# Keys and values of the first layer by node type, and table rows sent by indirect writes

## The chip, the cores and the metric

The kernel runs on one NeuronCore of a Trainium2 chip. The metric is the device time of one execution in microseconds (us), the median of several runs. A core has five engines that run side by side, each with its own queue of instructions in a fixed order: TensorE (PE, matrix products; PEld is its loading of weights), VectorE (DVE), ScalarE (ACT), GpSimd (POOL) and SyncE (SP, which only sends transfers here). Transfers between DRAM and the on-chip memory run on 16 DMA engines; they are sent from SyncE's queue (hardware_dynamic in the profile) or, where addresses come from data, from GpSimd's (software_dynamic: indirect gathers and indirect writes).

## The reference

A graph with N = 6250 nodes of 128 features and E = 200,000 edges sorted by target, with 16 node types and 32 edge types (RT), goes through two layers of attention over the edges with 8 heads of 16 features. `typed_linear` is a product whose matrix depends on the node's type.

```python
k = typed_linear(x, ntype, Wk).reshape(n, H, HS)
q = typed_linear(x, ntype, Wq).reshape(n, H, HS)
v = typed_linear(x, ntype, Wv).reshape(n, H, HS)
kT = jnp.einsum('nhd,htdo->nhto', k, Watt)
vT = jnp.einsum('nhd,htdo->nhto', v, Wmsg)
kw = kT[src, :, etype]
m = vT[src, :, etype]
a = jnp.einsum('ehd,ehd->eh', kw, q[dst]) * pri[:, etype].T / SQRT_D
att = edge_softmax(a, dst, n)
msg = (m * att[:, :, None]).reshape(-1, H * HS)
hag = jax.ops.segment_sum(msg, dst, num_segments=n)
h = jax.nn.silu(typed_linear(hag, ntype, Wa))
alpha = jax.nn.sigmoid(skip[ntype])[:, None]
h = h * alpha + x * (1.0 - alpha)
...
return (h - mu) * jax.lax.rsqrt(var + 1e-05) * g + b
```

After both layers come a product with `ff_w`, the addition of x and a normalization of each row.

## The kernel before

The nodes are cut into 49 tiles of 128. For each layer a table in DRAM holds, for every node and every edge type, the node's key and value under that edge type, 256 numbers; the table of layer 0 has one number more in each row, 32 times the node's place in the order by degree plus the edge type (1028 bytes a row, 206 MB in all). The edges of a target are then served by gathers out of that table (`gather`, L921): one indirect gather fetches one row for each of 128 targets into the tile `ring`.

The change touches what stands in front of the first such gather. Four pieces of it matter:

- **The edge check.** `load_edges` (L343 on) loads the edges, compares each target with its neighbour and sums the violations into `flag`; all engines load `flag` (L889) and branch over a sort that these inputs don't need. The first line behind the branch is the cast of `bounds` (L893).
- **The preparation.** `prepare` (from L510) finds each node's first edge: POOL writes the comparison tiles `cols` (L526), VectorE makes `less` from them (L531), TensorE counts, and `blk_i` (L541) names the block in which a node's edges begin. POOL gathers these blocks into `part` (L550, 50 gathers), VectorE compares them (`lt`, L558) and sums (`begin`, L560). Nodes are then ranked by degree: a 0/1 tile `hot` of 64 bins by 49 tiles (L599), two rounds of products into `total` and `ahead`, a running sum (L618), three passes over 3136 columns (L620 to L625). The places `pos_f` go to DRAM (`posd`) and come back turned, and `places` makes `place32` out of them (L507); from then on tables can be numbered. The records of all nodes are brought into that order by 49 pairs of `here` and `what` (L651, L653) with a product each, and `rec` is what POOL's gathers of `xg` (L683, x rows in that order, stored as `xperm`) and `idx_all` (L693, edge lists) read.
- **The typed keys and values.** `first_typed` and `one_typed` work on groups of two tiles: rows and types are loaded, transposed (L413), and for each of 16 types VectorE makes a masked copy `xm` (L426) and TensorE adds two products, with `wk` and `wv`, to one bank `kv` (L441). The groups run beside the preparation and beside the tables.
- **The tables.** `first_tables` goes over groups and tiles; for each tile `table_rows` makes 16 products of 512 columns (L474) with the relation blocks `bk`, `bv`, and ScalarE and VectorE copy each into a stage `st` (L483). A stage holds half a tile's rows, and there are four. VectorE writes the numbers (L847), and `send` sends each stage with two plain transfers of 1028 KB from SyncE (L872).

The program is written out by a planner. Each piece is a thread that yields an engine, a duration and what it waits for; the planner keeps a clock for every engine and emits the step that can begin first, ties going to the lower number in `RANK`. So the order of instructions on each engine is fixed by planned times; only the waits are settled on the chip. `relation_blocks` loads `bk`, `bv` and the scales `pr` by 24 small transfers and multiplies `bk` by `pr` on VectorE (L329, L330). `first_states` writes two DRAM tiles `state` from `init` (L878). The planner of the ring stage starts anew behind all this, with its own clock.

Of the kernel before, what the change touches and what calls it, by code (L numbers as in the profile page):

```python
# [31 lines left out]
F32 = mybir.dt.float32  # L32
# [6 lines left out]
P = 128  # L39
# [6 lines left out]
GL = 2  # L46
# [7 lines left out]
AHEAD = 2  # L54
KEPT = 16
STAGES = 4
# [11 lines left out]
RANK = dict(table=0, empty=0, gather=1, attend=1.6, prepare=2, mask=3, typed=3, late=4, query=1, behind=1.2, masks=1.4, early=1.8)  # L68
# [164 lines left out]
def gnn_kernel(ctx: ExitStack, tc: tile.TileContext, x, src, dst, etype, ntype, Wk, Wq, Wv, Wa,  # L233
# [17 lines left out]
    GROUPS = [list(range(a, min(a + GL, NTILE))) for a in range(0, NTILE, GL)]  # L251
# [86 lines left out]
    wk, wv = (load_typed(first, n, w[0]) for n, w in (("wk", Wk), ("wv", Wv)))  # L338
# [7 lines left out]
    def load_edges():  # L346

        landed = []
        for name, ap, fill in (("dst_i", dst, NODST), ("src_i", src, 0), ("typ_i", etype, 0)):
            us = yield "DVE", 1.4, ()  # L350
            edges[name] = t = pp.tile([P, EC], I32, tag=name, name=name)
            nc.vector.memset(t, fill)
# [39 lines left out]
        nc.sync.dma_start(out=csort[NBLK : NBLK + 1], in_=pad)  # L392

# [8 lines left out]
    def load_group(pool, tag, ap, t0, n, bufs):  # L402
        t = pool.tile([P, n, P], F32, tag=f"{tag}{n}", name=tag, bufs=bufs)
        nc.sync.dma_start(out=t, in_=ap[t0 * P : (t0 + n) * P].rearrange("(j p) d -> p j d", p=P))
        return t

    zeros = first.tile([P, GT * P], BF16, tag="zeros", name="zeros")
    nc.vector.memset(zeros, 0.0)

    def transposed(t, rows, n, needs):  # L410
        us = yield "PE", Work(n * P), needs
        for j in range(n):
            nc.tensor.transpose(t[:, j * P : (j + 1) * P], rows[:, j], ident)  # L413
        return t, us

    def typed(pool, tag, xT, types, M, cols, rows, opens, ends, clear, needs):


        ready, busy = [When() for _ in range(NT)], [When() for _ in range(NT)]
        masks, last = {}, [0.0]  # L420

        def mask():
            for t in range(NT):
                us = yield "DVE", dve_us(M), [*needs, busy[t - XM] if t >= XM else 0.0]
                xm = pool.tile([P, M], F32, tag=f"{tag}{M}", name=tag, bufs=XM)
                nc.vector.scalar_tensor_tensor(xm, types[:, :M], float(t), xT[:, :M], op0=ALU.is_equal, op1=ALU.mult)  # L426
                masks[t], ready[t].us, last[0] = xm, us, us

        plan.spawn(mask(), RANK["mask"])
        for t in range(NT):  # L430
            busy[t].us = yield "PE", Work(M * (len(cols) + len(rows))), [ready[t], clear]
            xm = masks.pop(t)
            if t == 0:
                for a in opens:
                    nc.tensor.matmul(a, zeros[:, :P], zeros[:, : a.shape[-1]], start=True, stop=False)
            todo = [(w, acc[:, :M], None) for w, acc in cols]
            todo += [(w, acc[:, c : c + P], slice(c, c + P)) for w, acc in rows for c in range(0, M, P)]
            for i, (w, to, c) in enumerate(todo):
                last_of = t == NT - 1 and i in ends
                if c is None:  # L440
                    nc.tensor.matmul(to, w[:, t], xm, start=False, stop=last_of)  # L441
                else:
                    nc.tensor.matmul(to, xm[:, c], w[:, t], start=False, stop=last_of)
        return busy[-1].us, last[0]

    def copied(pool, tag, acc, M, bufs, needs):
        us, e = yield ("ACT", "DVE"), (act_us(M), dve_us(M)), needs
        t = pool.tile([P, M], F32, tag=f"{tag}{M}", name=tag, bufs=bufs)
        if e == "ACT":
            nc.scalar.copy(t, acc[:, :M])  # L450
        else:
            nc.vector.tensor_copy(t, acc[:, :M])
        return t, us
# [35 lines left out]
    ap = early.enter_context(tc.tile_pool(name="ap", bufs=2))  # L489
# [3 lines left out]
    placed, known, searched = When(), When(), When()  # L493
# [7 lines left out]
    def places(posn, got):  # L501

        us = yield "PE", Work(P), [got]
        to = tabs[0]
        nc.tensor.transpose(to[:, :NTILE], posn, ident[:NTILE, :NTILE])
        us = yield "DVE", 0.3, [us]
        nc.vector.tensor_scalar(place32, to[:, :NTILE], float(RT), None, op0=ALU.mult)  # L507
        known.us = us

    def prepare():  # L510
        stage = ExitStack()
# [5 lines left out]
        yield "DVE", 0.3, ()  # L517
        ones_b = pp.tile([P, P], BF16, tag="ones_b")
        nc.vector.memset(ones_b, 1.0)
# [22 lines left out]
        searched.us = us  # L542
        begin = pp.tile([P, NC1], F32, tag="begin")
        seen = [us]
        for t0 in range(0, NC1, CB):
# [3 lines left out]
            for t in range(n):  # L549
                nc.gpsimd.indirect_dma_start(  # L550
                    out=part[:, t], out_offset=None, in_=dsort,
                    in_offset=bass.IndirectOffsetOnAxis(ap=blk_i[:, t0 + t : t0 + t + 1], axis=0),
                    bounds_check=NBLK - 1, oob_is_err=False)
# [19 lines left out]
        yield "SP", 1.6, ()  # L573
        nt_i = pp.tile([P, NTILE], I32, tag="nt_i")
        full = N // NTILE
        nc.vector.memset(nt_i, -1)
        nc.sync.dma_start(out=nt_i[:112], in_=ntype[: 112 * NTILE].rearrange("(p t) -> p t", t=NTILE))
# [980 lines left out]
```

## Time and profile before

| what | us |
|---|---|
| median of 3 runs | 6403.71 (6397.04 to 6416.18) |
| the profiled execution | 6422.69 |
| its span in the trace | 6420.9 |
| from the start to `blk_i` | 64.9 |
| first sends of the table | 216.89 |
| first gather into the ring | 879.07 |
| from there to the end | 5541.8 |

In rows of the trace a line names an instruction by engine, line, operation and tile (`out<-in`), with its duration; [ ] at its end holds how long the engine was idle before it and what ended the wait. A row "x8" joins eight instructions that follow each other. The granted clock (PEclk) is the share of TensorE's full speed that the chip granted in a stretch: 1.00 is 2.4 GHz and 0.5 is 1.2 GHz. A DMA share is the mean busy share of the 16 DMA engines.

### The profile page before, as it was taken

The numbers are of one execution on the slowest core, as the hardware profiler recorded it, in microseconds if no ns is written. First come the engines' busy times: TensorE is split into PE (matmuls) and PEld (weight loads), VectorE is DVE, ScalarE is ACT, GpSimd is POOL, SyncE is SP. The second block draws the span as 40 slices with busy tenths as digits, with TensorE's granted clock in tenths as the row PEclk, the third lists the DMA queues.
The fourth block names the chain that finished last, engine by engine and source line by source line (L and its number), as shares of the span: only waits on it lengthen the run. The fifth ranks groups of instructions, "written<-read, shape, count | busy, mean of one in ns | idle before, by whom it ended". The sixth has DMA issues, their size and how long they took to land. (4 is left out here: it accounts for less than half of the span.)

```text
span 6420.9 us, 36014 instructions
## 1 busy us (share of the span) xinstructions
PE 2871.1 (45%) x8591; PEld 1387.5 (22%) x8599; DVE 3917.8 (61%) x5664; ACT 935.9 (15%) x1921; POOL 3427.8 (53%) x3428
## 2 busy tenths in 40 slices
PE   5887941354555545655655664122232222221112
PEld 4553520121222212221222232010011111110002
DVE  7864637456555655565565563656466666666667
ACT  0333310020211202211111232000000000000001
POOL 4022036555546556555554524766676666767662
PEclk8998975566665566666666776565565565555555
DMA  4696873252525525434444544433333333333331
GB/s 118 264 388 252 338 262 87 74 179 75 186 90 168 178 79 188 168 104 158 157 128 150 181 171 178 117 89 103 103 104 93 98 97 97 99 104 99 94 97 34
DMA packets 323165, 923.16 MB, mean 144 GB/s; under 512 B 82759, under 2 KB 169844, under 8 KB 285312
## 3 DMA queue, kind: packets, MB, share of 16 engines
q0 software_dynamic: 161888, 438.75, 23.6%
q1 hardware_dynamic: 161056, 482.05, 19.9%
q8 instruction: 68, 1.11, 0.1%
q14 instruction: 153, 1.25, 0.1%
HBM read 486.99 MB, written 433.57 MB: 143 GB/s over the span
## 5 line engine op out<-in xcount | busy, mean ns | idle before, releaser
L921 POOL DMA_INDIRECT ring<-table,idx_all x3208 | 3208.5, 1000 | 2498.5 <-issue 2000.9
L1072 DVE SCALAR_TENSOR_TENSOR xm<-types,xb 128x512 f32<-128x512 f32 (+3 forms) x880 | 490.5, 589 | 665.9 <-remote 317.3
L483 ACT COPY st<-tab 128x512 f32<-128x512 f32 x1146 | 613.2, 597 | 1123.6 <-PE tab L474 532.8
L992 DVE TENSOR_REDUCE add<-ring 128x128 f32<-128x2048 f32 (+11 forms) x270 | 745.4, 2761 | 48.4 <-remote 28.6
L474 PE MATMUL tab<-bv,vT 32*128 32x512 f32 x1568 | 478.2, 797 | 172.5 <-issue 89.1
L474 PE MATMUL tab<-bk,kT 32*128 32x512 f32 x1568 | 455.2, 795 | 212.5 <-issue 159.6
L961 DVE TENSOR_TENSOR ring<-ring,sb 128x2048 f32<-128x2048 f32 (+12 forms) x266 | 459.9, 1729 | 143.0 <-DMA ring<-table,idx_all 126.5
L963 DVE TENSOR_REDUCE sb<-ring 128x128 f32<-128x2048 f32 (+11 forms) x270 | 470.7, 1743 | 58.1 <-remote 41.5
L483 DVE COPY st<-tab 128x512 f32<-128x512 f32 x422 | 275.1, 686 | 349.5 <-PE tab L474 176.9
L1080 PE MATMUL av<-xm,wa 128*128 128x512 f32 (+3 forms) x736 | 358.2, 641 | 273.3 <-DVE xm L1072 214.2
L1080 PE MATMUL tab<-xm,wq 128*128 128x512 f32 (+3 forms) x416 | 250.2, 755 | 508.9 <-DVE xm L1072 177.4
L988 DVE TENSOR_TENSOR ring<-ring,sb 128x2048 f32<-128x2048 f32 (+11 forms) x270 | 467.4, 1731 | 0.0
L1080 PE MATMUL av<-xm,wq 128*128 128x512 f32 (+3 forms) x544 | 285.6, 670 | 266.5 <-DVE xm L1072 215.9
L1080 PE MATMUL ak<-xm,wk 128*128 128x512 f32 (+3 forms) x480 | 247.2, 601 | 108.7 <-DVE xm L1072 91.0
L441 PE MATMUL kv<-xm,wk 128*128 128x256 f32 (+1 forms) x800 | 268.1, 419 | 43.4 <-DVE xm L426 42.8
L1234 ACT COPY sb<-qr 128x128 f32<-128x128 f32 x97 | 26.3, 271 | 1691.6 <-DVE sb L963 988.5
L1080 PEld LDWEIGHTS av<-xm,wa 128*128 128x128 f32 x736 | 155.3, 234 | 468.6 <-DVE xm L1072 272.0
L474 PEld LDWEIGHTS tab<-bv,vT 32*128 32x128 f32 x1568 | 170.5, 222 | 373.4 <-issue 178.9
L441 PE MATMUL kv<-xm,wv 128*128 128x256 f32 (+1 forms) x800 | 248.7, 394 | 0.0
L1080 PEld LDWEIGHTS tab<-xm,wq 128*128 128x128 f32 x416 | 105.7, 285 | 642.9 <-DVE xm L1072 217.5
L474 PEld LDWEIGHTS tab<-bk,kT 32*128 32x128 f32 x1568 | 158.6, 221 | 394.8 <-issue 249.9
L1080 PE MATMUL av<-xm,wv 128*128 128x512 f32 (+3 forms) x480 | 234.3, 573 | 0.0
(216 smaller groups left out, 2875.8 us busy)
## 6 DMA issues: line engine op xcount, KB each, us to landing
table<-st SPq DMA_DIRECT2D x196, 1028.0 KB
table<-st SPq DMA_DIRECT2D x98, 2048.0 KB
ring<-table,idx_all POOLq DMA_INDIRECT x3208
state<-init SPq DMA_DIRECT2D x2, 3528.0 KB
state<-state SPq DMA_DIRECT2D x98, 72.0 KB
types<-tyrow SPq DMA_DIRECT2D x20, 256.0 KB
rows<-in_x_dram SPq DMA_DIRECT2D x24, 128.0 KB
types_i<-in_node_type_dram SPq DMA_DIRECT2D x24, 128.0 KB
```

Of the source, the lines that this page charges most:

```text
L441: nc.tensor.matmul(to, w[:, t], xm, start=False, stop=last_of)
L474: nc.tensor.matmul(tab, cT[here, nodes], blk[here, t0 : t0 + per].rearrange("p t o -> p (t o)"), start=True, stop=True)
L483: (nc.scalar.copy if e == "ACT" else nc.vector.tensor_copy)(to, tab.rearrange("p (t o) -> p t o", o=width))
L921: nc.gpsimd.indirect_dma_start(out=ring[:, place], out_offset=None, in_=tables[layer], in_offset=bass.IndirectOffsetOnAxis(ap=idx[:, s : s ...
L961: nc.vector.tensor_tensor(kk, kk, q[:, None, :].to_broadcast([P, m, P]), op=ALU.mult)
L963: nc.vector.tensor_reduce(sc[:, s0 : s0 + m], kk.rearrange("p s (h d) -> p s h d", h=H), axis=AX.X, op=ALU.add)
L988: nc.vector.tensor_tensor(vv.rearrange("p s (h d) -> p s h d", h=H), vv.rearrange("p s (h d) -> p s h d", h=H), sc[:, s0 : s0 + m, :, None ...
L992: nc.vector.tensor_reduce(add, vv.rearrange("p s c -> p c s"), axis=AX.X, op=ALU.add)
L1072: nc.vector.scalar_tensor_tensor(xm[:, :M], types[:, :M], float(t), xT[:, :M], op0=ALU.is_equal, op1=ALU.mult)
L1080: nc.tensor.matmul(to[:, :M], w[:, t], xm[:, :M], start=(t == 0), stop=(t == NT - 1))
L1234: nc.scalar.copy(q, rows[0][:, j])
```

## The change

The first layer's typed products are done once for each type, not once for each type and pair of tiles. `ranks`, a new thread ahead of the edge check, counts the types with the same ranking that the degrees use (`positions`, now a function) and leaves `nids`, the nodes' numbers in order of type, and `starts`, the column at which each type begins. `typed_rows` gathers the rows of x in that order with 49 indirect gathers on POOL, transposes them into one tile `xT` of 6272 + 512 columns, loads `starts` into registers of TensorE, ScalarE and VectorE, and makes for each type two products of 512 columns at the register's column; the copies into `kT` and `vT` (6784 columns each) go to the same column, and a later type overwrites what an earlier one wrote beyond its end. 512 columns hold any type of at most 512 nodes; for a larger one `any_table` under a branch behind the tables writes all of the table anew in the old way.

Since a tile's 128 nodes now lie anywhere in the table, a tile is sent by one indirect write on POOL, 128 rows of 32,896 bytes, out of a stage that holds a whole tile; there are two stages in place of four halves. The places in the order by degree are known in that same order of nodes (`slots`), so `place32` is made of them at once, and `posd` is written by 49 indirect writes of one number per partition and read back in plain order for `rec`. Degrees are brought into the order of types by 49 small products (`moved`). The records of types by slot (`kinds_of_slots`) become a thread of the lowest rank, `xg` gets three buffers, and `wk` and `wv` are loaded behind the edges.

```diff
-RANK = dict(table=0, empty=0, gather=1, attend=1.6, prepare=2, mask=3, typed=3, late=4, query=1, behind=1.2, masks=1.4, early=1.8)
+RANK = dict(table=0, rows=2.5, empty=0, gather=1, attend=1.6, prepare=2, mask=3, typed=3, late=4, query=1, behind=1.2, masks=1.4, early=1.8)
...
+    def positions(pool, hot, to, needs, ends=None):
...
+        for i, c in enumerate(parts):
+            w = c.stop - c.start
+            us = yield "PE", Work(w // 4), needs
+            n_ps = tabs[i % 3]
+            nc.tensor.matmul(n_ps[:, :w], upper, flat[:, c], start=True, stop=True)
+            yield "DVE", dve_us(w), [us]
+            nc.vector.tensor_tensor(upto[:, c], upto[:, c], n_ps[:, :w], op=ALU.add)
...
+    def moved(what, cols, needs):
+
+        to = prep_bank()
+        us = yield "PE", Work(NTILE * (cols // 4 + 16)), needs
+        for t in range(NTILE):
+            nc.tensor.matmul(to[:, :cols], here_all[:, t], what[:, t], start=(t == 0), stop=(t == NTILE - 1))
+        return to, us
...
+    def typed_rows():
+
+        yield "POOL", 0.0, [ranked]
...
+            for j, t in enumerate(g):
+                got = yield "POOL", GATHER_US, [took[-2]]
+                on_pool[0] = None
+                nc.gpsimd.indirect_dma_start(
+                    out=rows[:, j], out_offset=None, in_=x,
+                    in_offset=bass.IndirectOffsetOnAxis(ap=nids[:, t : t + 1], axis=0),
+                    bounds_check=N - 1, oob_is_err=False)
+            _, us = yield from transposed(xb, rows, n, [got + 2.5])
+            took.append(us)
+            us = yield "ACT", act_us(n * P), [us]
+            nc.scalar.copy(xT[:, g[0] * P : (g[0] + n) * P], xb[:, : n * P])
...
+        for t in range(NT):
+            for i, (w, to, e) in enumerate((("wk", kT, "ACT"), ("wv", vT, "DVE"))):
+                b = banks[(2 * t + i) % 3]
+                us = yield "PE", Work(WIN), [us, empty[-3]]
+                nc.tensor.matmul(b, edges[w][:, t], xT[:, ds(at["PE"][t], WIN)], start=True, stop=True)
+                done = yield e, act_us(WIN), [us]
+                (nc.scalar.copy if e == "ACT" else nc.vector.tensor_copy)(to[:, ds(at[e][t], WIN)], b)
+                empty.append(done)
+        columned.us = done
...
+        for t in range(NTILE):
+            us = yield "POOL", GATHER_US, [us]
+            s = nc.gpsimd.indirect_dma_start(
+                out=posd, out_offset=bass.IndirectOffsetOnAxis(ap=nids[:, t : t + 1], axis=0), in_=slots[:, t : t + 1],
+                in_offset=None, bounds_check=NP - 1, oob_is_err=False)
+            apart(s, "posd")
...
+    def first_tables():
         yield "SP", 0.0, [known]
+        yield "SP", 0.0, [columned]
+        xstage.close()
...
+        for t in range(NTILE):
+            u = t % STAGES
+            st, gone = sts[u], last[u]
+            halves = yield from table_rows(tabs, [st[:, : RT // 2], st[:, RT // 2 :]], kT, vT, t, bk, bv, [columned], [gone] * 2)
+            us = yield "DVE", 0.2, [gone]
+            nc.vector.tensor_scalar(st[:, :, ROW], kinds_r, place32[:, t : t + 1], None, op0=ALU.add)
+            last[u] = When()
+            plan.spawn(send(t, st, [us, *halves[0], *halves[1]], last[u]), 0)
+
+    def send(t, st, filled, done):
+        us = yield "POOL", GATHER_US, filled
+        s = nc.gpsimd.indirect_dma_start(
+            out=tables[0].rearrange("(n t) c -> n (t c)", t=RT),
+            out_offset=bass.IndirectOffsetOnAxis(ap=nids[:, t : t + 1], axis=0),
+            in_=st.rearrange("p t c -> p (t c)"), in_offset=None, bounds_check=NP - 1, oob_is_err=False)
+        apart(s, "table0")
+        done.us = (yield "DMA", 10.6, [us]) + 2.0
...
-    def send(dest, c, st, filled, done):
-        us = yield "SP", 0.8, filled
-        for s0 in (0, RT // 4):
-            nc.sync.dma_start(out=dest[:, c * RT // 2 + s0 :][:, : RT // 4], in_=st[:, s0 : s0 + RT // 4])
-        done.us = (yield "DMA", 5.4, [us]) + 2.0
...
+    stage.close()
     keep.close()
+    common = nc.values_load(most_of[0:1, 0:1], min_val=0, max_val=NP)
+    with tc.If(common > WIN):
+        any_table()
     early.close()
```

What moves on the engines shows at three places. On VectorE ahead of the branch (`here_all` and `what_all` are the 0/1 tiles of the new ranking, `many` its counts) the kernel before has:

```order
L426 SCALAR_TENSOR_TENSOR xm<-types,xb 128x256 x2
L383 CAST flag<-pb 1x1
L389 SCALAR_TENSOR_TENSOR comb<-src_i,typ_i 128x1564
L426 SCALAR_TENSOR_TENSOR xm<-types,xb 128x256 x9
L838 MEMSET bk 128x1024
L838 MEMSET bv 128x1024
L889 TENSOR_LOAD flag
L890 COMPARE_AND_BRANCH
```

and the changed kernel, in front of its own load of `flag`:

```order
L862 MEMSET bv 128x1024
L326 TENSOR_SCALAR pr<-pr 128x32
L327 TENSOR_TENSOR bk<-bk,pr 128x1024
L564 TENSOR_SCALAR what<-what_all,lane 128x49x49
L565 TENSOR_TENSOR what<-what_all,lanes 128x49x49
L366 CAST dst_f<-dst_i 128x1564
L367 CAST dst_f<-prior 128x1
L370 TENSOR_TENSOR tmp<-dst_f 128x1564
L373 TENSOR_REDUCE bad<-tmp 128x1
L569 COPY parts<-pb 128x98
L570 SCALAR_TENSOR_TENSOR nids<-parts 128x49
L379 CAST flag<-pb 1x1
```

The scaling of `bk`, which stood behind `blk_i` before, now stands ahead of the edge check, and the edge check behind it. On POOL, from the branch to the gathers of `part`, the kernel before has:

```order
L515 IOTA nid 128x50
L526 IOTA cols 128x640 x10
L550 DMA part<-dsort,blk_i 128x391 x50
L590 IOTA bins 128x64
L593 IOTA lanes 128x128
```

and the changed kernel:

```order
L663 IOTA nid 128x50
L671 IOTA cols 128x640
L590 DMA rows<-in_x_dram,nids 128x128 x4
L671 IOTA cols 128x640 x5
L590 DMA rows<-in_x_dram,nids 128x128 x4
L671 IOTA cols 128x640
L590 DMA rows<-in_x_dram,nids 128x128 x4
L671 IOTA cols 128x640 x3
L590 DMA rows<-in_x_dram,nids 128x128 x4
L695 DMA part<-dsort,blk_i 128x391 x5
L590 DMA rows<-in_x_dram,nids 128x128 x4
L695 DMA part<-dsort,blk_i 128x391 x5
```

The last two rows then alternate until 49 gathers of x rows and 50 of `part` are issued. Further on, POOL has in the kernel before no sends of the table; SyncE has them (four stages, two transfers each):

```order
L627 DMA posd<-pos_f 128x49
L630 DMA posn<-posd 49x128
L789 DMA rows<-in_x_dram 128x2x128
L810 DMA types_i<-in_node_type_dram 128x256
L872 DMA table_60<-st_116 128x2056 x2
L872 DMA table_60<-st_117 128x2056 x2
L872 DMA table_60<-st_118 128x2056 x2
L872 DMA table_60<-st_119 128x2056 x2
```

and in the changed kernel POOL has, behind the last `part`:

```order
L732 IOTA bins 128x64
L748 DMA posd<-slots,nids 6272x1 x22
L887 DMA table_60<-st_1467,nids 6272x8224
L748 DMA posd<-slots,nids 6272x1 x8
L887 DMA table_60<-st_1468,nids 6272x8224
L748 DMA posd<-slots,nids 6272x1 x9
L887 DMA table_60<-st_1467,nids 6272x8224
L748 DMA posd<-slots,nids 6272x1 x8
L887 DMA table_60<-st_1468,nids 6272x8224
```

The sends of the table stand in one queue with the writes of `posd`, and later with the gathers of `xg` (packs of four, a pack to each two sends) and of `idx_all` (packs of 17, 16, 13 and 3, each behind a send).

## Rows read from the trace of the kernel before

**Rows 1.** The page: busy us of each engine, share of the span, instructions

```profile
PE 2871.1 (45%) x8591; PEld 1387.5 (22%) x8599; DVE 3917.8 (61%) x5664; ACT 935.9 (15%) x1921; POOL 3427.8 (53%) x3428
```

**Rows 2.** The timeline where the tables end (start, us, engine, line, operation); one group

```profile
878.63 0.91 DVE L1286 MEMSET bk<- 128x1024 f32 x1 [17.61 <-DMA table<-st]
879.07 1.01 POOL L921 DMA_INDIRECT ring<-table,idx_all  x1 [339.62 <-issue]
...
L921 POOL DMA_INDIRECT ring<-table,idx_all x3208 | 3208.5, 1000 | 2498.5 <-issue 2000.9
```

**Rows 3.** The timeline about the edge check, a product of 256 columns among it

```profile
36.73 4.77 SPq L320 DMA_DIRECT2D bk<-in_L_gnn_Watt_dram  x8
...
38.03 0.59 PE L441 MATMUL kv<-xm,wv 128*128 128x256 f32 x2
...
38.50 0.17 DVE L893 CAST bounds<-dst_i 128x4 f32<-128x4 int32 x1 [0.72 <-SPq L890]
...
45.79 3.72 SPq L325 DMA_DIRECT2D pr<-in_L_gnn_pri_dram  x8
```

**Rows 4.** Groups of 0 to 209 (busy, mean ns), then the timeline at `blk_i`

```profile
L531 DVE TENSOR_SCALAR less<-cols,bounds 128x640 bf16<-128x640 f32 x40 | 23.4, 652 | 0.8 <-POOL cols L526 0.8
...
L526 POOL IOTA cols<- 128x640 f32 x10 | 9.1, 918 | 11.8 <-DVE less L531 11.8
...
64.74 0.19 DVE L541 CAST blk_i<-blk 128x50 int32<-128x50 f32 x1
```

**Rows 5.** The gathers of `part`: their group, single ones on POOL, the last `lt`

```profile
L550 POOL DMA_INDIRECT part<-dsort,blk_i x50 | 61.9, 1237 | 30.1 <-issue 12.5 <-DVE lt L558 10.8 <-DVE types L821 4.7
...
88.93 1.00 POOL L550 DMA_INDIRECT part<-dsort,blk_i  x1 [10.78 <-DVE lt L558]
...
92.84 2.99 POOL L550 DMA_INDIRECT part<-dsort,blk_i  x1 [0.30 <-issue]
...
151.51 1.00 POOL L550 DMA_INDIRECT part<-dsort,blk_i  x1 [0.30 <-issue]
...
154.85 2.20 DVE L558 TENSOR_TENSOR lt<-part,nid 128x1955 bf16<-128x1955 int32 x1 [1.62 <-DMA part<-dsort,blk_i]
```

**Rows 6.** VectorE about the known places, then SyncE's first sends of the table

```profile
192.51 5.71 DVE L625 TENSOR_REDUCE pos_f<-total 128x49 f32<-128x3136 f32 x1
...
206.40 0.20 DVE L507 TENSOR_SCALAR place<-tab 128x49 f32<-128x49 f32 x1
...
216.89 3.71 SPq L872 DMA_DIRECT2D table<-st  x4
```

**Rows 7.** Windows (busy us of five engines, granted clock, DMA share, GB/s), then VectorE

```profile
340.00:360.00 20.00, 14.26 (x62) 8.35 (x64) 8.79 (x19) 5.78 (x11) 0.00 (x0) 0.72 1.02 405
...
500.00:520.00 20.00, 2.73 (x7) 1.25 (x5) 0.68 (x3) 0.00 (x0) 15.19 (x16) 0.59 0.35 118
...
220.00:300.00 80.00, 79.95 (x438) 44.23 (x435) 69.98 (x181) 36.27 (x68) 0.56 (x2) 1.00 1.01 415
...
700.00:860.00 160.00, 158.43 (x881) 94.66 (x873) 110.37 (x248) 65.53 (x124) 0.00 (x0) 1.00 0.88 354
...
852.97 0.37 DVE L847 TENSOR_SCALAR st<-kinds_r,place 128x16 f32<-128x16 f32 x2
...
859.15 0.37 DVE L847 TENSOR_SCALAR st<-kinds_r,place 128x16 f32<-128x16 f32 x2
```

**Rows 8.** The timeline beside the gathers of `idx_all`: table products, sends

```profile
475.66 1.14 PE L474 MATMUL tab<-bv,vT 32*128 32x512 f32 x8
...
481.54 61.59 SPq L872 DMA_DIRECT2D table<-st  x8
...
484.44 2.09 PE L474 MATMUL tab<-bk,kT 32*128 32x512 f32 x8
```

**Rows 9.** Groups of the stretch 209 to 879: the typed work

```profile
L441 PE MATMUL kv<-xm,wk 128*128 128x256 f32 (+1 forms) x614 | 201.0, 410 | 2.3 <-DVE xm L426 1.9 <-issue 0.2
...
L426 DVE SCALAR_TENSOR_TENSOR xm<-types,xb 128x256 f32<-128x256 f32 (+1 forms) x304 | 118.1, 408 | 59.3 <-PE kv L441 23.9 <-remote 21.3 <-PE tab L474 13.2
```

More of the change, by code (lines that the diff above doesn't have):

```diff
@@ L413, in transposed @@
             nc.tensor.transpose(t[:, j * P : (j + 1) * P], rows[:, j], ident)
[L414 to L452, printed above, removed]
         return t, us
@@ new lines, in typed_rows @@
+    def typed_rows():
+        yield "POOL", 0.0, [ranked]
+        us = yield "DVE", 0.7, ()
+        xT = xp.tile([P, NP + WIN], F32, tag="xT", name="xT")
+        nc.vector.memset(xT[:, NP:], 0.0)
+        took = [0.0, 0.0]
+        for g in WIDE:
+            n = len(g)
+            if g[-1] == NTILE - 1:
+                yield "DVE", 0.5, [took[-2]]
+            rows = xp.tile([P, GT, P], F32, tag="rows", name="rows", bufs=2)
+            if g[-1] == NTILE - 1:
+                nc.vector.memset(rows, 0.0)
+            for j, t in enumerate(g):
[9 more added lines that the diff above has]
+            nc.scalar.copy(xT[:, g[0] * P : (g[0] + n) * P], xb[:, : n * P])
+        at = {}
+        for eng, e in ((nc.tensor, "PE"), (nc.scalar, "ACT"), (nc.vector, "DVE")):
+            yield e, (Work(300) if e == "PE" else 1.0), [us]
+            regs = [eng.alloc_register(f"start{e}{i}") for i in range(NT)]
+            eng.load(regs, starts[0:1, :NT])
+            at[e] = [nc.s_assert_within(eng.snap(r), 0, NP, skip_runtime_bounds_check_because="clamped when it was made")
+                     for r in regs]
+        empty = [0.0] * 3
+        banks = [kvb, *tabs[3:]]
+        for t in range(NT):
[7 more added lines that the diff above has]
+        columned.us = done
@@ L761, in prepare @@
-        stage.close()
-    on_pool = [None]
     def apart(s, group):
@@ L832, in gnn_kernel @@
-    free, relations = [0.0] * STAGES, []
+    tabs, kvb, xb = [bank(ps, f"tab{i}") for i in range(5)], bank(ps, "kv"), bank(ps, "xb")
+    free, relations, stages, sent = [0.0] * 2 * STAGES, [], [], {}
     def relation_blocks():
@@ L896, in gnn_kernel @@
     with tc.manual_schedule():
-        plan.spawn(first_typed(range(AHEAD, len(GROUPS))), RANK["typed"])
-        plan.spawn(first_tables(range(len(GROUPS))), RANK["table"])
+        plan.spawn(typed_rows(), RANK["rows"])
+        plan.spawn(first_tables(), RANK["table"])
         plan.spawn(prepare(), RANK["prepare"], flagged.us + 6.0)
```

416 lines of the change are left out of this document (219 added, 197 removed).

## The prediction

> **What bounds the kernel now.** I read the page first, then windows of 20 us, then the timeline at the seams. [Rows 1]: one core, no engine busy for more than 61% of the span of 6420.9 us, so no engine sets the whole. The trace falls in two parts. From 879.07 on [rows 2] the ring gathers of the two layers run, 3208 of 1000 ns each, for 5541 us; the change touches none of their code. What it can move is the time of that first gather. In front of it the last step is a transfer: VectorE, with the last fill done, waits 17.61 us for `table<-st`, and the first gather starts 0.44 us after it is released [rows 2]. So the question is one sum: when does the last table tile land.
>
> Before, that stretch has a lead-in (until 216.89, the first sends, [rows 6]) and the building of 49 tiles of 4.21 MB (128 nodes x 32 kinds x 1028 B). The building has several limits [rows 7]: 220 to 300 the transfers are full (415 GB/s, DMA share 1.01; a tile costs 4.21/0.415 = 10.1 us); 500 to 520 little moves (118 GB/s, and less in the 20 us behind it) while the 49 gathers of `idx_all` run back to back (POOL busy for 15.19 of 20) and eight sends hold SyncE 61.59 us [rows 8]; 700 to 860 TensorE is the limit (158.43 of 160 us busy at a granted clock of 1.00, 354 GB/s).
>
> **What the change takes away.** The typed work beside the tables: 614 records with `wk` (201.0 us), as many with `wv`, and 304 masks (118.1 us) in 209 to 879 [rows 9]. That frees the TensorE-bound stretch: at 415 instead of 354 GB/s, 160 us of it would take 136. The near standstill, some 40 us, goes too, if the sends on POOL's own queue don't stop as SyncE's did. All 49 tiles at 10.1 us are 495 us, where the building took 879 - 217 = 662. That is 167 us to be won at most, less what is added.
>
> **What it adds to the lead-in**, on the clock of the trace.
> 1. VectorE now scales `bk` (`pr`, `bk<-bk,pr`) ahead of the edge check; it waits for 24 small loads that SyncE issues from 36.73 to 49.51, 12.8 us [rows 3]. Their issue waits on the memset of `bk`, which comes some 10 us earlier now (nine masks are gone, seven comparisons of 896 columns come): loads landed near 41. Then come two products of 2401 columns, the edge check (a comparison and a sum of 1564 columns, some 2 us each by `lt`'s 2.20 for 1955, [rows 5]), the casts, `flag`, `comb`: `bounds` near 58 instead of 38.50: **+20** (10 to 25). All engines stand behind that branch, so nothing hides this wait.
> 2. Sixteen gathers of x rows stand between the `cols` on POOL: 16 x 1.30 + 10 x 0.92 = 30.0 us where VectorE's 23.44 us ruled [rows 4]. From `bounds` to `blk_i` 35 instead of 26: **+9** (7 to 12).
> 3. The other 33 gathers stand between the 50 of `part`, each 1.00 us with 0.30 us behind it [rows 5]: 33 x 1.30 = 43, less some 10 us in which POOL had waited for `lt` before (10.78 at 88.93): **+33** (28 to 45). Last `lt` near 217, not 154.85.
> 4. From the last `lt` to the known places took 51.6 us (154.85 to 206.40) [rows 5, 6]. The round trip of positions through DRAM goes (198.22, the reduction's end, to 206.40: 8 us); 49 `moved` products, a product of 2401 columns and seven additions out of PSUM come, and eight copies of columns. I take **0** (-8 to +8): places near 269. The loads of `wk` and `wv`, later on SyncE, and two memsets of 6784 columns on POOL lie ahead of the branch or beside the comparisons; without that cover they cost what the loads took together, under 10 us.
> 5. Only half of the typed products are done by then. Eight kinds x 2 products of 512 columns, each twice one of 256 columns that took 0.59 [rows 3], so at most 1.18: at most 18.9 us in a row, and I take 17, to 286; one fill of 6.2 to 293. Meanwhile 22 writes of `posd` hold POOL from 269 for 28.7 us, so the first send goes at **299**, where before it was 217: **+82** in all.
>
> **The building after.** A tile needs a fill F, an issue I, a transfer T, and a landing R before its stage is free. F is 6.2 us at the granted clock of 1.00 (`st<-kinds_r` at 852.97 and 859.15, [rows 7]); at half clock a quarter's eight records take 2.09 instead of 1.14 [rows 8], so F is 6.2 + 4 x 0.95 = 10.0. I is 1.30, R 2.3 (the gather of 151.51 ends 152.51, its reader starts 154.85, [rows 5]). With two stages a tile costs max(T, (F+I+T+R)/2): 10.1 at the full clock, (10.0+1.3+10.1+2.3)/2 = 11.9 at the half. TensorE is then busy for 6.2 of 10.1 us; rows of that share show a clock between the levels (14.26 of 20 us at 0.72 in 340 to 360, [rows 7]). I take 10.6.
> - tiles 1 to 3, with 8, 9 and 8 `posd` writes between the sends (11.7, 13.0 and 11.7 us with the send ahead of each): fourth send at 335
> - 46 tiles x 10.6 = 488, and I + R = 3.6: 827
> - `state<-init`, two tiles of 6272 x 144 numbers, 7.2 MB at 415 GB/s: 17
> - `xg` and `xperm`, 6.4 MB: 15 if nothing hides it, and 0.5 us per tile is free: 9
> - `idx_all` now stands on POOL between sends in packs of 17, 16, 13 and 3 (1.30 us each, by the busy 15.19 of 20 for 16 of them in 500 to 520, [rows 7]): 22, 21 and 17 us against T = 10.1: 12 + 11 + 7, less what queues: 27
>
> Sum **880**: the first ring gather comes 1 us later than before, which is no change. The additions of 82 us and the packs eat the gain. The skipped fallback at the seam (a register load, a branch) lies behind the landing of the last table, which no engine can pass, and costs 0 to 3 us.
>
> A rule of the Trainium skill speaks against sending by POOL: eight of the 50 `part` gathers took 1.80 to 2.99 us instead of 1.00 (the longest and the mean of 1237 ns in [rows 5]), each while `lt` of 2.2 us ran on VectorE. "DMA: Bandwidth & Descriptors", section "SWDGE vs HWDGE vs iDMA", says that GpSimd writes such descriptors into SBUF, which VectorE can lock it out of, and that sends from SyncE are immune. The trace agrees for `part`; no row here shows it for a send of 4 MB. By that rule I would be up to 3.3 instead of 1.30, and the sum the third rival's.
>
> **The rivals.**
> - *Faster:* the building is bound by transfers alone: T = 10.1 for each tile, packs of `idx_all` hidden behind two queued sends, row traffic in gaps. 335 + 46 x 10.1 + 3.6 + 17 + 9 = 829, or 843 with half the packs: 36 to 50 us less, about 6360. For it: F+I+R = 9.8, just under T. Against it: one late fill costs at once, with two stages only.
> - *Slower, the loop of two stages:* TensorE rests 4 us of each 10 and falls to the half clock; a tile costs 11.9 us. 46 x 1.3 = 60 us on the forecast: 6465. It decides from the point where F+I+R exceeds T, that is from a fill of 6.5 us. For it: 340 to 360, where TensorE was busy for 14.26 of 20 us, shows 0.72 [rows 7]. Against it: a longer fill itself raises TensorE's share.
> - *Slower, POOL locked out by VectorE's copies:* each send costs 2 us more (2.99 for 1.00), and at half of that in the loop, 46 x 1.0 = 46: 6451. Against it: a copy of `st` is short: eight on either engine fit in a fill of 6.2 us, while `lt` takes 2.2.
> - *The change doesn't do what it says:* a kind with over 512 nodes, and the whole table is built again by the fallback. 49 turns of a fill of at least 6.2 us would be 304 us more. The mean of a kind is 6250/16 = 391, with types drawn alike the spread is 19, and it needs 121 above the mean.
>
> **How the numbers follow.** The sum stands against the profiled execution, 6422.69 us, which is 19 above the median of the runs shown, 6403.71; the shift of the first gather is put on the median: 6403.71 + 1 = 6405. A change of 0.3% (19 us) is about what a measurement of this kernel can tell from none. Chances: forecast 0.36 (a shift within 19 us), faster rival 0.34, half clock 0.20, locked POOL 0.09, fallback 0.01. So faster 0.34, same 0.36, slower 0.30. The range takes in the faster rival (6403.71 - 50, rounded to 6350) and the half clock with all else as forecast (6465); left out is less than 2 in 10: the fallback, both slow rivals at once, a lead-in longer by over 30 us.
>
> **What would show it.** `bounds` near 58, `blk_i` near 93, last `lt` near 217, places near 269, the first `table` send on POOL near 299. In 350 to 600 windows of 390 to 415 GB/s mean the transfer bounds; 330 to 360 with a clock under 0.8 means the loop of two stages does. A mean of the L887 sends of 1.0 or of 3 us tells whether POOL is held. `idx_all` in three packs, each with a dip of the transfers. If the ring phase, 5541 us from first gather to end, moves by over 10 us, the premise that only the first gather's time counts is wrong.

## The result and the profile after

The changed kernel is **slower**: 6615.17 us, median of four runs (6611.38 to 6620.93), against 6409.94 us for the kernel before (median of four, 6397.04 to 6418.30). The ratio is 1.0323, 95% interval 1.0301 to 1.0344. The forecast of 6405 and its range of 6350 to 6465 both miss it.

The profiled execution took 6611.38 us, its span is 6609.3. First the page of the kernel after: busy us of each engine, share of the span, instructions. It answers to [rows 1]: TensorE lost 1452 matmuls and 160 us of work, and the kernel became longer by 188 us, so the loss is idle time.

```profile
PE 2711.5 (41%) x7139; PEld 1243.2 (19%) x7139; DVE 3817.5 (58%) x5238; ACT 937.9 (14%) x1899; POOL 3590.4 (54%) x3577
```

Then the seam, from the timeline of the kernel after (start, us, engine, line, operation; in brackets the idle time before and what ended it). It answers to [rows 2]:

```profile
1064.63 0.91 DVE L1351 MEMSET bk<- 128x1024 f32 x1 [22.57 <-issue]
1065.26 1.05 POOL L986 DMA_INDIRECT ring<-table,idx_all  x1 [15.65 <-issue]
```

The first ring gather starts at 1065.26 instead of 879.07: 186.2 us later, of the 188.4 by which the span grew. From there to the end both kernels take the same (5544.0 and 5541.8 us). So the loss lies ahead of this gather, and the question is where in those 186 us.

**The lead-in came nearly as forecast.** Timeline of the kernel after, VectorE and SyncE's queue (SPq), up to the known places; it answers to [rows 3 to 6]:

```profile
34.63 4.04 SPq L317 DMA_DIRECT2D bk<-in_L_gnn_Watt_dram  x8
...
47.94 0.18 DVE L326 TENSOR_SCALAR pr<-pr 128x32 f32<-128x32 f32 x1 [12.26 <-DMA pr<-in_L_gnn_pri_dram]
...
62.72 0.17 DVE L954 CAST bounds<-dst_i 128x4 f32<-128x4 int32 x1 [2.52 <-SPq L951]
...
101.41 0.19 DVE L686 CAST blk_i<-blk 128x50 int32<-128x50 f32 x1
...
225.07 2.20 DVE L703 TENSOR_TENSOR lt<-part,nid 128x1955 bf16<-128x1955 int32 x1 [2.63 <-DMA part<-dsort,blk_i]
...
266.82 0.19 DVE L744 TENSOR_SCALAR place<-slots 128x49 f32<-128x49 f32 x1
```

**The first send did not.** Timeline of the kernel after on POOL, behind the known places:

```profile
269.52 0.99 POOL L748 DMA_INDIRECT posd<-slots,nids  x1 [1.44 <-DMA posd<-slots,nids]
271.95 0.97 POOL L748 DMA_INDIRECT posd<-slots,nids  x1 [1.44 <-DMA posd<-slots,nids]
...
319.70 0.97 POOL L748 DMA_INDIRECT posd<-slots,nids  x1 [1.42 <-DMA posd<-slots,nids]
320.97 0.97 POOL L887 DMA_INDIRECT table<-st,nids  x1 [0.30 <-issue]
322.25 0.97 POOL L748 DMA_INDIRECT posd<-slots,nids  x1 [0.30 <-issue]
333.38 0.97 POOL L748 DMA_INDIRECT posd<-slots,nids  x1 [10.17 <-DMA posd<-slots,nids]
...
349.53 0.97 POOL L887 DMA_INDIRECT table<-st,nids  x1 [0.30 <-issue]
...
408.14 0.97 POOL L887 DMA_INDIRECT table<-st,nids  x1 [0.30 <-issue]
```

Each write of `posd` waits 1.4 us for the one ahead to land, so it costs 2.40 us from start to start, not 1.30. Behind a send of the table it is worse: the write at 322.25 is issued at once, but stands in the same queue behind 4.2 MB, and the write at 333.38 waits 10.17 us for it. While POOL stands there, no table tile can be sent.

**The sends of the table wait for each other too.** POOL and, at 952.90, VectorE in the tail of the building, where nothing else is left to do:

```profile
940.96 0.96 POOL L887 DMA_INDIRECT table<-st,nids  x1 [11.65 <-DVE st L435]
953.67 0.96 POOL L887 DMA_INDIRECT table<-st,nids  x1 [11.75 <-DVE st L435]
966.34 0.96 POOL L887 DMA_INDIRECT table<-st,nids  x1 [11.71 <-DVE st L435]
...
1048.64 0.96 POOL L887 DMA_INDIRECT table<-st,nids  x1 [13.95 <-DVEq L1084]
...
952.90 1.29 DVE L435 COPY st<-tab 128x512 f32<-128x512 f32 x2 [4.12 <-DMA table<-st,nids]
```

The releaser named for POOL is VectorE's copy; but that copy itself had waited for a landing (`table<-st` at 952.90) and fills the next tile. The tile that goes at 953.67 had its last copy at 948.09; what it waited for is the landing, and the windows show it. Windows of the kernel after (busy us of PE, PEld, DVE, ACT, POOL, then granted clock, DMA share, GB/s):

```profile
350.00:420.00 70.00, 15.86 (x58) 8.51 (x58) 9.90 (x20) 8.74 (x16) 19.90 (x21) 0.57 0.43 181
540.00:700.00 160.00, 121.11 (x387) 63.84 (x383) 70.25 (x121) 56.33 (x103) 36.54 (x37) 0.56 0.82 334
830.00:910.00 80.00, 41.31 (x129) 21.74 (x129) 33.67 (x144) 17.93 (x32) 53.81 (x53) 0.54 0.52 197
940.00:1060.00 120.00, 70.35 (x246) 37.67 (x246) 43.16 (x72) 35.69 (x64) 8.67 (x9) 0.64 0.74 317
945.00:950.00 5.00, 4.96 (x20) 2.26 (x14) 2.52 (x5) 1.78 (x3) 0.00 (x0) 0.76 1.12 480
952.00:955.00 3.00, 1.46 (x6) 1.35 (x9) 1.29 (x2) 1.57 (x3) 0.96 (x1) 0.50 0.00 0
956.00:964.00 8.00, 5.83 (x26) 2.84 (x22) 3.75 (x7) 2.62 (x5) 0.00 (x0) 0.90 1.07 461
```

Between 952 and 955 nothing moves: one tile has landed, and only then the next is issued. A tile costs 12.7 us (953.67 to 966.34), of which the transfer needs some 9 (4.21 MB at 461 to 480 GB/s). In 350 to 420 the queue is at 181 GB/s, and TensorE busy for 15.86 of 70 us: that is the stretch of the `posd` writes.

The cause, which e1 to e3 put to the test, is in `apart`, the helper through which both kinds of write go. It tells the scheduler that writes to one buffer don't depend on each other, except (`kept`) on the POOL write directly ahead. That one dependence is enough: it becomes a wait for the landing. A gather in between breaks the chain, since it leaves no write to keep (`on_pool[0] = None`): where packs of `xg` stand between the sends, only every second send waits (677.44 was idle for 2.79 us, 694.08 for 15.63).

### The profile page after: what moved, and what is told of

Its sections match the earlier page's. It is cut to its first block, busy times and chain, and to the rows that moved or that the text cites. A ratio compares the mean times of both kernels' runs of the same rounds, so it can differ in the third digit from the quotient of the medians.

```text
span 6609.3 us, 32375 instructions
## 1 busy us (share of the span) xinstructions
PE 2711.5 (41%) x7139; PEld 1243.2 (19%) x7139; DVE 3817.5 (58%) x5238; ACT 937.9 (14%) x1899; POOL 3590.4 (54%) x3577
## 5 line engine op out<-in xcount | busy, mean ns | idle before, releaser
L426 PE MATMUL tab<-bv,vT 32*128 32x512 f32 x1568 | 689.9, 947 | 396.5 <-ACT st L435 249.6
L426 PE MATMUL tab<-bk,kT 32*128 32x512 f32 x1568 | 618.9, 934 | 204.9 <-issue 120.6
L435 DVE COPY st<-tab 128x512 f32<-128x512 f32 x437 | 291.1, 688 | 602.6 <-DMA table<-st,nids 274.8
L426 PEld LDWEIGHTS tab<-bv,vT 32*128 32x128 f32 x1568 | 250.2, 264 | 685.4 <-ACT st L435 395.1
L426 PEld LDWEIGHTS tab<-bk,kT 32*128 32x128 f32 x1568 | 236.8, 260 | 410.9 <-issue 216.7
L887 POOL DMA_INDIRECT table<-st,nids x49 | 48.4, 987 | 442.9 <-DVE st L435 346.4
L1145 PE MATMUL tab<-xm,wa 128*128 128x512 f32 (+2 forms) x224 | 122.3, 687 | 188.6 <-DVE xm L1137 116.7
```

What stands on the lines that cost most here:

```text
L426: nc.tensor.matmul(tab, cT[here, nodes], blk[here, t0 : t0 + per].rearrange("p t o -> p (t o)"), start=True, stop=True)
L435: (nc.scalar.copy if e == "ACT" else nc.vector.tensor_copy)(to, tab.rearrange("p (t o) -> p t o", o=width))
L887: s = nc.gpsimd.indirect_dma_start(out=tables[0].rearrange("(n t) c -> n (t c)", t=RT), out_offset=bass.IndirectOffsetOnAxis(ap=nids[:, t ...
L1145: nc.tensor.matmul(to[:, :M], w[:, t], xm[:, :M], start=(t == 0), stop=(t == NT - 1))
```

## The experiments

Twelve runs were made, on three chips; b0 and c1 to c4 repeat kernels. The ratio of each is to the kernel before on its own chip. On the chip of e1 to e4 the kernel before takes 5240 us, since the part from the first ring gather on takes some 4413 us there instead of 5544; so their ratios can't be put beside the 1.0323. What carries the argument is the start of the first ring gather. The differences e1 to e3, e2 to e3, e3 to e4, those among e5 to e7 and c1 to c3 are between runs of one chip. The changed kernel did not run on the chip of e1 to e4; in its two traces the gather starts at 1065.26 and 1065.01 (c1), and e1 to e3 are put beside that.

**e1: no dependence between the writes of `posd`.**

```diff
-        kept = [on_pool[0]] if on_pool[0] is not None else []
+        kept = [on_pool[0]] if on_pool[0] is not None and group != "posd" else []
```

> The changed kernel, but a write of posd no longer waits until the write ahead of it has landed (the declared dependence on the instruction ahead is dropped for posd; the rows written are distinct); sends of the table still wait for each other. Theory (two chains of landings, posd's and the table's): posd from start to start 1.30 instead of 2.40 us, first send near 297 instead of 321, fourth near 335 instead of 408, pace of the sends after that unchanged (12.7 us where they stand alone), first ring gather near 992 instead of 1065, some 6542 us. Rival (posd is held in the queue behind the table's data whatever it waits for): only the 24 us ahead of the first send are won, 6590.

POOL in e1, from the places on:

```profile
269.25 0.99 POOL L748 DMA_INDIRECT posd<-slots,nids  x1 [0.30 <-issue]
...
296.09 0.97 POOL L887 DMA_INDIRECT table<-st,nids  x1 [0.30 <-issue]
...
341.36 0.97 POOL L887 DMA_INDIRECT table<-st,nids  x1 [0.30 <-issue]
...
997.54 1.05 POOL L986 DMA_INDIRECT ring<-table,idx_all  x1 [16.50 <-DVE bk L1351]
```

The writes now cost 1.30 us, the first send goes at 296.09 and the fourth at 341.36 (320.97 and 408.14 before). First ring gather 997.54, 68 us earlier where 73 were expected; ratio 1.0327 (1.0309 to 1.0344). The rival, only 24 us, is out.

**e2: no dependence between the sends of the table** (the same line, `group != "table0"`).

> The changed kernel, but a send of the table no longer waits until the send ahead of it has landed; posd keeps its chain. Theory (two chains): lead-in as in the changed kernel, fifth send near 430, then 10.6 us for a tile instead of 12.4 to 14: first ring gather near 955, some 6505 us; DMA share of windows behind 930 near 1.0 instead of 0.74. Rival (the loop of two stages at a clock between the levels sets the pace, not the landing of the other stage's send): sends go on at 12 us or more, the time within 20 us of the changed kernel's 6615.

```profile
1016.60 1.05 POOL L986 DMA_INDIRECT ring<-table,idx_all  x1 [17.67 <-DVE bk L1351]
```

Ratio 1.0358 (1.0341 to 1.0375). The gather comes 49 us earlier, where 110 were expected. The chain was there, but behind it stood another limit: 22 tiles from 540.04 to 800.13, 11.8 us to a tile, not 10.6. That is most of what the rival said, which put the pace at 12 us or more.

**e3: both.**

> The changed kernel with both chains dropped. Theory (two chains): the sum of the prediction as it stood, first ring gather near 880, some 6430 us, that is 185 us under the changed kernel. Rival (loop of two stages): as with posd alone freed, near 6540.

```profile
944.09 1.05 POOL L986 DMA_INDIRECT ring<-table,idx_all  x1 [17.10 <-DVE bk L1351]
```

First ring gather 944.09, ratio 1.0233 (1.0216 to 1.0250). With the other chain gone already, the chain of `posd` is worth 72.5 us (1016.60 to 944.09) and that of the table 53.5 (997.54 to 944.09). The two don't add up: against 1065 both together give 121 us of the 186. But 880 was expected, and 64 us were still to be found. Windows of e3 (columns as above) show the two places:

```profile
524.00:700.00 176.00, 147.50 (x492) 79.73 (x492) 83.44 (x139) 69.80 (x125) 48.02 (x48) 0.60 0.97 394
700.00:830.00 130.00, 75.65 (x261) 40.65 (x260) 56.43 (x182) 35.98 (x65) 59.26 (x58) 0.62 0.68 271
830.00:925.00 95.00, 79.39 (x269) 43.55 (x268) 46.09 (x78) 38.32 (x68) 7.70 (x8) 0.61 0.88 377
```

TensorE is at a granted clock of 0.6, near half, and TensorE and the transfers wait in turn: 11.4 us to a tile from 857.63 to 926.03 (six tiles in 68.4). And where `idx_all` is gathered, in 700 to 830, the transfers fall to 271 GB/s.

**e4: e3, and the scaling of `bk` behind the branch**, so that the edge check does not wait for `pr`.

```diff
-        scale_blocks(bk, load_scales(first, 0))
+    def scaled():
+        yield "DVE", 1.5, ()
+        scale_blocks(relations[0], relations[2])
```

> Both chains dropped, and the relation blocks are scaled by pr behind the branch, among the comparisons, not ahead of the edge check. Theory (the wait for pr's landing is on the path that leads to the first send): bounds near 51 instead of 62.7, everything up to the first send 11 to 12 us earlier than with both chains dropped, and 8 to 12 us less in all. Rival (the wait for pr covers other waits, so that the edges or the comparisons wait in its place): bounds earlier but the first send within 3 us of the kernel with both chains dropped.

`bounds` came at 55.17 instead of 62.72 (51 expected), the first send at 279.57 instead of 295.29, the first ring gather at 931.09: 13 us earlier, where 8 to 12 were expected. The wait for `pr` was on the path. Ratio 1.0202 (1.0185 to 1.0219). Its VectorE shows waits that stand in order ahead of copies of `st`:

```profile
350.73 0.19 DVE L501 CAST pos<-pos_f 128x49 int32<-128x49 f32 x1 [10.84 <-DMA pos_f<-posd]
...
478.11 0.97 DVE L647 TENSOR_TENSOR pick<-one_of,sk 128x784 f32<-128x784 f32 x1 [9.91 <-DMA sk<-in_L_gnn_skip_dram]
```

Each stops VectorE's copies for some 10 us: the load of `pos_f`, issued at 341.75, is there only at 350.73, and the copies of `st` stand behind it in the order.

**b0: the kernel before**, once more with its trace, on the chip of the next three.

> The kernel before, unchanged, for its trace on the chip of these runs, where the ring gathers have been quicker than in the profile of before. Theory (the standstill of 490 to 545, with its remote waits, belongs to that first profile and not to the kernel): no window under 200 GB/s between 300 and 800, first ring gather 40 to 60 us ahead of 879. Rival (it belongs to the gathers of idx_all beside sends from SyncE): the same standstill, first ring gather within 10 us of 879.

First ring gather 878.38, and its near standstill is there: 109 GB/s in 490 to 545. The theory failed and the rival held. So the first gather of the kernel before is where it was, and the steps below stand against it.

**e5: e4 with three stages** (`STAGES = 3`; two 0/1 tiles of the ranking go to a pool that is closed before the stages are opened, to make room).

> As e4 (chains dropped, scaling late), but three stages for table tiles; the 0/1 tiles of the ranking are given up before the tables to make room. Theory (with two stages the loop of fill, issue, transfer and landing sets the pace, 11.2 to 11.6 us a tile in e4): 10.1 to 10.4 us a tile in 530 to 700 and behind 830, first ring gather 25 to 40 us ahead of e4's 931. Rival (the transfer itself takes 11 us when sent by indirect writes): the pace stays above 11, first gather within 8 us of e4.

First ring gather 912.38, against 931.09 and 932.78 for e4 (c3, below), both on other chips: 19 to 20 us, less than the 25 to 40 expected. Behind the packs of `idx_all` the pace came as expected, six tiles from 827.38 to 888.08, 10.1 us to a tile, so the rival (a transfer of 11 us) is out; but from 536.57 to 701.77 a tile still took 11.0 us, with the transfers full (408 GB/s, share 0.99, in 530 to 700). Time 1.0006 of the kernel before (0.9983 to 1.0030), though the gather is 34 us behind that of b0: between single executions on this chip the ring phase, from the first gather to the end, runs from 5409 (e7) to 5485 us (b0), so a time doesn't resolve a step of this size.

**e6: e5, with the waits spread.** The scheduler, which had reckoned 2.5 and 3 us for the two small loads, reckons 24; and between two gathers of `idx_all` it leaves 1.5 us to other work of POOL.

```diff
-            us = yield "DVE", 2 * dve_us(NTILE * NT), [us + 3.0]
+            us = yield "DVE", 2 * dve_us(NTILE * NT), [us + 24.0]
...
-        us = yield "DVE", 2.0, [got + 2.5]
+        us = yield "DVE", 2.0, [got + 24.0]
...
-            us = yield "POOL", GATHER_US, ()
+            us = yield "POOL", GATHER_US, [paced]
+            paced = us + 1.5
```

> As e5, and the gathers of idx_all are spread by 2.8 us each instead of standing in packs of up to 17, and two waits of VectorE (the read of pos_f, the load of sk) are placed 20 us later in its order. Theory (packs of idx_all cost 27 us or more, the two VectorE waits of 10.84 and 9.91 us hold the copies of the stages behind them): first ring gather 40 to 60 us ahead of e5's, no window under 330 GB/s between 320 and the end. Rival (with three stages there is slack that hides both): within 15 us of e5.

First ring gather 870.94, 41 us earlier. The two windows of 720 to 790, first of e5, then of e6:

```profile
720.00:790.00 70.00, 34.29 (x117) 18.31 (x111) 30.05 (x135) 15.32 (x27) 43.65 (x42) 0.60 0.44 153
```

```profile
720.00:790.00 70.00, 59.05 (x214) 32.94 (x212) 38.98 (x84) 28.77 (x52) 27.21 (x27) 0.70 1.00 410
```

In e5 POOL has 42 instructions there, one of them a send (744.35) and most of the others gathers of `idx_all`, and 153 GB/s move; in e6, with 27 in the same time, the transfers are full. Which of the two edits gave the 41 us shows in the traces. The 37th send, ahead of the packs, first of e5, then of e6, and with it e6's two waits:

```profile
713.71 0.99 POOL L889 DMA_INDIRECT table<-st,nids  x1 [6.28 <-issue]
```

```profile
714.01 1.01 POOL L891 DMA_INDIRECT table<-st,nids  x1 [2.53 <-DVE st L435]
...
364.74 0.19 DVE L501 CAST pos<-pos_f 128x49 int32<-128x49 f32 x1 [9.60 <-DMA pos_f<-posd]
...
541.87 0.97 DVE L647 TENSOR_TENSOR pick<-one_of,sk 128x784 f32<-128x784 f32 x1 [9.94 <-DMA sk<-in_L_gnn_skip_dram]
```

Up to the 37th send e6 is no earlier than e5, and VectorE still waits 9.60 and 9.94 us. The last send goes at 888.08 in e5 and at 847.10 in e6. So the 41 us come where the packs stand, and the later places in the order did not take the two waits away: what these cost was not tested. In 470 to 520 e6 still has 300 GB/s, where no window under 330 was expected. Time 0.9955 (0.9929 to 0.9982).

**e7: e6, with the gathers of `part` ahead of the last 33 of the x rows**, and the `posd` writes reckoned 1.2 us apart.

```diff
-                got = yield "POOL", GATHER_US, [took[-2]]
+                got = yield "POOL", GATHER_US, [took[-2], *([listed] if g[0] >= 4 * GT else [])]
```

> As e6, and the 33 gathers of x rows that stood between the gathers of part come behind them; writes of posd are spread too. Theory (the rows gathers lengthen the chain to the known places by 33 x 1.30 us, and products of types fit behind the places): places near 213 instead of 256, first send near 255 instead of 280, first ring gather 20 to 27 us ahead of e6's. Rival (the typed products, now wholly behind the places, take all of it back): first send within 6 us of e6's.

The places come at 225.54, 31 us earlier than in e6 (256.37), and the first send no earlier: 285.93 against 286.41. The rival held. POOL, and TensorE's typed products, in e7:

```profile
247.59 2.08 PE L611 MATMUL tab<-xT,wv 128*128 x2 [3.62 <-issue]
251.85 2.07 PE L611 MATMUL kv<-xT,wk 128*128 x2 [2.18 <-DVE vT L613]
...
265.60 1.02 PE L611 MATMUL kv<-xT,wk 128*128 x2
...
285.93 0.97 POOL L892 DMA_INDIRECT table<-st,nids  x1 [29.24 <-ACT st L435]
```

POOL is done with the 23 `posd` writes that stand ahead of the first send and waits 29.24 us for the first fill, since the products now stand behind the rows. They run from 232 to 277; two in a row take 2.07 us in 250 to 262, at a granted clock of 0.50, and 1.02 in 262 to 277, at 0.94. First ring gather 859.59, 11 us earlier than in e6, where 20 to 27 were expected; the first send does not explain the 11, and their cause stays open. Time 0.9949 (0.9914 to 0.9984).

**c1 to c4: the changed kernel, the kernel before, e4 and e7 on one chip**, a third one, to see whether the steps hold there.

> The changed kernel as it is, beside the next three on one chip, since the four runs without the two chains of waits and the three later ones came from two chips. Theory (the first ring gather is a sum of waits that lie in the code): 1065 here on any chip, within 5 us; what differs between chips is the ring phase alone, 4413 or some 5450 to 5540 us. Rival (the chips differ in the building too, and steps between runs of two chips are worth nothing): first gather off 1065 by over 10 us.

> The kernel before on the chip of the other three. If the ring phase is some 4413 us here: its own run of 5240 on such a chip, less 4413 and 2, would put the first ring gather near 825, and the near standstill of 490 to 545 (109 GB/s on the other kind of chip) should then be missing or shorter, with few waits put down to no engine (remote). If the ring phase is 5450 or more: first gather 878 to 879 once more and the standstill there.

> The changed kernel without the two chains of waits for a landing and with the scaling behind the branch, once more, beside the changed kernel and the last version on one chip. Theory: first ring gather 931 (within 5), so 134 us before that of the changed kernel on the same chip. Rival (part of the gain was the chip's): under 115 us.

> The last version (no chains, scaling late, three stages, spaced waits, gathers of part first) on the chip of the other three. Theory: first gather 860 (within 5) on any chip. If the ring phase is some 4413 here: a time of 5275, slower than the kernel before by 0.6% (5240), because the kernel before loses its standstill on such a chip and the last version has none to lose. If the ring phase is 5450 or more: 0.995 of the kernel before, as it was.

In this order the first ring gathers start at:

```profile
1065.01 1.05 POOL L986 DMA_INDIRECT ring<-table,idx_all  x1 [15.66 <-issue]
```

```profile
878.68 1.01 POOL L921 DMA_INDIRECT ring<-table,idx_all  x1 [338.84 <-issue]
```

```profile
932.78 1.06 POOL L989 DMA_INDIRECT ring<-table,idx_all  x1 [17.09 <-DVE bk L1354]
```

```profile
867.52 1.00 POOL L993 DMA_INDIRECT ring<-table,idx_all  x1 [5.48 <-DVE low L1090]
```

The changed kernel, the kernel before and e4 are where they were, within 2 us: without the two chains and the wait for `pr` the gather comes 132 us earlier, 134 expected. The last version came 8 us later than on its first chip (859.59), outside the 5 allowed, so a step of that size between runs of two chips says nothing. It took 0.9994 of the kernel before (0.9973 to 1.0015), where 0.995 was expected. Between the two chips, its gain is 0 to 0.5%. That this is near the forecast of no change bears nothing out: the forecast's sum had neither the waits that were taken out nor the third stage and the spread packs that were put in.

## Why the prediction was wrong

**The steps that held.** That only the time of the first ring gather counts: 186.2 of 188.4 us. The lead-in: `bounds` 62.72 (58 forecast), `blk_i` 101.41 (93), last `lt` 225.07 (217), places 266.82 (269). Three of the four came 5 to 8 us late (the loads of `pr` were there at 47.94, not near 41), and the step from there to the places was 10 us short.

**The step that failed is "22 writes of `posd` hold POOL from 269 for 28.7 us", and with it "with 8, 9 and 8 `posd` writes between the sends (11.7, 13.0 and 11.7 us)".** Both price a write at its issue of 1.30 us. It costs 2.40, and 11.1 us (322.25 to 333.38) right behind a send. So the first send went at 320.97 instead of 299, and the three steps to the fourth took 87 us instead of 36: it went at 408.14 instead of 335, 73 us late. e1 takes that away: its fourth send goes at 341.36.

**The second failed step is "a tile costs max(T, (F+I+T+R)/2)".** It lets one tile be sent while the other lands; with sends that wait for each other a tile costs T + R + I, which with 9 + 2.3 + 1.3 = 12.6 is the 12.7 us of the tail. From the fourth send to the 49th (1048.64) the kernel took 640 us, where the forecast's terms (45 x 10.6, and 53 for `state`, `xg` and `idx_all`) gave 530. Of these 110 us the table's chain is some 53 (e3 against e1).

**The rest, 64 us in e3, is the pace of the loop and the packs, put too low.** Set beside the forecast's terms, e3 loses 5 us up to the fourth send (340.31), 33 from there to the 35th (728.18: 31 tiles of 12.5 us, where 10.6 and 26 for `state` and `xg` were forecast), 10 in the four steps across the packs of `idx_all` (79.3 us to 807.48, forecast 69.4), 13 in the last ten tiles (11.9 us each) and 4 behind them. The loop of two stages at the low clock was a rival with 0.20, at 11.9 us to a tile; behind the chains it was there, at 11.4 to 11.9 (a third stage: 19 us back). VectorE's waits for `pos_f` and `sk`, some 10 us each, the sum did not have at all; what they cost stays open. The packs were in the sum with 27 us; spread out, they give back 41 from e5 (e6). The wait for `pr`, 12.26 us, was in the sum too, in the +20, but as unavoidable: e4 gets 13 us back. 121 + 13 + 19 + 41 = 194, the whole way from the changed kernel to e6 (1065 to 871).

**The other rivals.** "Transfers alone" did not come about, though T itself was put too high: a lone send moves at 461 to 480 GB/s, not 415. "POOL locked out by VectorE's copies" is refuted for the sends, by three groups of the kernel after (busy, mean ns | idle before): the sends, the gathers of x rows, VectorE's copies into `st`:

```profile
L887 POOL DMA_INDIRECT table<-st,nids x49 | 48.4, 987 | 442.9 <-DVE st L435 346.4 <-issue 45.2 <-ACT st L435 25.9
L590 POOL DMA_INDIRECT rows<-in_x_dram,nids x49 | 61.6, 1257 | 14.4 <-issue 14.1 <-DVE less L676 0.3
...
L435 DVE COPY st<-tab 128x512 f32<-128x512 f32 x437 | 291.1, 688 | 602.6 <-DMA table<-st,nids 274.8
```

A send takes 987 ns, with some nine copies on VectorE to a tile (437 for 49); the gathers of x rows, beside VectorE's comparisons, take 1257. The rule of the Trainium skill ("DMA: Bandwidth & Descriptors", "SWDGE vs HWDGE vs iDMA"), that VectorE in its 2-port perf mode locks GpSimd out of the SBUF state to which it writes descriptors, would fit the gathers; on the sends, for which I had weighed it, the trace shows no such hold, and in which mode VectorE's copies run no trace here shows. The fallback did not run: its 49 turns do not appear.

**Why it was missed.** The `order` rows ahead of the prediction show that `posd` writes and sends share a queue, and the diff shows that both go through `apart`, whose kept dependence stands in the kernel's text. The prediction counted what POOL issues and never asked what each write waits for. It had the price of a landing, too: it took R as 2.3 us for the stages. One landing for each of 22 writes would have added some 24 us to the first send (22 x 1.1, the difference that was measured), enough to put the forecast outside "no change".

## What to carry to other kernels

Where a write is declared independent of all others but one, that one still costs a landing for each write, and in a queue shared with large transfers the landing of everything ahead: price a chain of indirect writes by the landing, unless the trace shows them issued back to back. A limit that is found behind another (here the loop of two stages behind the chain) gives its time back only when the first is gone, so forecast with all of them and not with the largest. Small gathers that stand in a pack between two large sends of one queue starve the transfers (153 GB/s against 410 when they were spread): space them out. And where a planned order is changed to hide a wait, read in the new trace whether the wait is gone; in e6 both were still there.

## What the runs showed of the hardware

- The kernel before takes 5240 us on one chip and 6324 to 6410 in the other sets of runs (medians). For the changed kernel's variants the building is the same (e4: 931.09 and 932.78), and the ring phase, the same code, takes 4413 us (e2 to e4) or 5409 to 5544. Why the chips differ stays open. The kernel before may gain in the building too on the quick chip: 5240 less 2 and 4413 leaves 825 instead of 879. No trace of it was taken there, so that stays open; if it is so, the ratios of e1 to e4 stand against a better kernel before than those of the later runs.
- Where each `posd` write (128 numbers of 4 bytes) waits for the landing of the one ahead, the next starts 2.40 us after it in an empty queue, and 11.1 us after it (322.25 to 333.38) behind one send of 4.2 MB in the same queue.
- The issue of an indirect write takes 0.97 us on POOL, whether each of its 128 rows is 4 bytes or 33 kB.
